# Moving one pair of pooled sums to GpSimd and reordering the hand-over to the second recurrence of a recommender kernel

## The chip, the cores and the metric

The kernel runs on one NeuronCore of a Trainium2 chip. The metric is device time in microseconds (us), from one launch; the times given are medians of several runs. A core has five engines with queues of their own, which run side by side and wait for one another through semaphores: TensorE (PE in the profile; PEld is its loading of weights), VectorE (DVE), ScalarE (ACT), GpSimd (POOL) and SyncE (SP, which here only issues DMAs).

## The reference

1024 sequences of 100 steps of 128 numbers pass a GRU; attention weights over its states pool them into one vector of 128 numbers for each sequence; then a second recurrence (AUGRU) runs over the GRU's states, and its update gate is scaled by numbers taken from the pooled vectors. Cut to what matters:

```python
_, gru_seq = jax.lax.scan(gru_step, h0, jnp.swapaxes(item_historical_embedding, 0, 1))
keys = jnp.swapaxes(gru_seq, 0, 1)
...
attn = jax.nn.softmax(score, axis=1)[..., 0]
pooled = jnp.einsum('bt,btd->bd', attn, keys)
att_seq = pooled.T[:T]

def augru_step(h, inp):
    x_t, a_t = inp
    ti = jnp.concatenate([h, x_t], axis=-1)
    r = jax.nn.sigmoid(ti @ aug_Wr.T + aug_br)
    u = jax.nn.sigmoid(ti @ aug_Wu.T + aug_bu)
    h_hat = jnp.tanh(jnp.concatenate([h * r, x_t], axis=-1) @ aug_Wh.T + aug_bh)
    u = a_t[:, None] * u
    h_new = (1.0 - u) * h + u * h_hat
    return (h_new, h_new)
_, aug_seq = jax.lax.scan(augru_step, h0, (jnp.swapaxes(keys, 0, 1), att_seq))
```

The state at each sequence's own last step, with other features, goes through a small network that gives one score for each sequence. Note `att_seq`: number t of a sequence's pooled vector is its weight at step t of the second recurrence. So the second recurrence needs the whole pooling finished, and then the pooled numbers by step instead of by sequence.

## The kernel before, in words

All is held in fp32. The 1024 sequences are worked on as two halves of 512; a tile is 128 partitions by 512 columns, and a matmul of 512 columns is issued as two instructions.

**First phase** (`gru_phase`). A loop over 100 steps does both halves of the GRU, the attention scores, a running softmax and the pooled sums. The states are written to `keys_d` in HBM, transposed in blocks of 32, as rows that can be gathered later: `keys_d[0]` has steps 0 to 3, `keys_d[1]` steps 4 to 11, and so on. `Half.pool(count, eng, cs)` (line 671) takes pending items of one half off its list `todo` and issues them on the engine `eng` for the columns `cs`: an item without a step rescales the sum (line 683), each other item is a pair, a product at line 693 and a sum at line 694. `count` limits the pairs.

The end of the phase (lines 1075 to 1145) is written out by hand, in the order in which the engines get it. The columns 0 to 3 of the pooled vectors (`soon`) are finished first, since steps 0 to 3 need them; from them, by matmuls, come `chosen` (the weights of those steps, sorted) and the first state `h3`. Then come the other 28 columns (`rest`): GpSimd does the rescaling and one pair of half 0 (line 1135); VectorE finishes half 1 (line 1137), SP issues four stores of its pooled rows to `pooled_d` (line 1140); then VectorE does half 0's last pair, and SP issues four stores of half 0. SP last issues a 1 MB store of half 0's keys (line 663), and GpSimd gathers the eight remaining blocks of half 0's key rows for steps 4 to 11 (`more_early`, line 193). A gather is an indirect DMA of 128 rows that GpSimd issues; each takes its queue's place.

**Second phase** (`augru_phase`, line 1147). It sits behind a branch on a value that was read from HBM. For each step t and half i, `half_step(t, i)` (line 1271) does this:

- PE: closes the `ph` gate of the half step before (line 1260, from `r`), closes `pr` and `pu` of its own, then opens `pr`, `ph`, `pu` of the half step after (line 1256, from the keys).
- ACT: tanh and two sigmoids (lines 1268, 1284, 1285).
- DVE: products with the other half's new state and with this half's gates (lines 1290, 1292, 1294, 1298, 1301).

PSUM banks are handed out by hand. The opened gates take them in turn from `ring`, which begins 6, 3, 1, 0, 2, 5, 4. One more bank (`pa`, a single buffer) serves transposes and other short matmuls. `SPARE` is bank 0.

What the first steps add:

- `chosen_rows` makes the weights of step 1; `store_chosen(i, p)` (line 1190) makes those of steps 0 to 3 in the bank `p`, ACT copies them (line 1193), SP stores them to `att_d` and loads the rows for steps 2 and 3 (line 1220). Both halves are called in `half_step(1, 1)`, half 0 in bank 0 and half 1 in `pa`.
- `load_key(t, i)` makes the keys of a step: for steps 1 to 3 by four transposes on PE into `pa` (line 1238) and a copy on ACT (line 1239), later by transposes on DVE (line 1245) from the gathered rows, which all have to be there.
- `gather_weights(i)` (line 1177): four gathers of sorted rows from `pooled_d` (line 158). They wait for all eight stores.
- `store_weights(i)` (line 1198), in `half_step(2, 1)` for half 0 and `half_step(3, 0)` for half 1: DVE multiplies the gathered rows by a mask (line 1203), PE transposes them into `pa` (line 1205), DVE copies them (line 1207), SP stores them to `att_d` and loads the row of step 4.
- From step 2 on, `load_att(t + 2, i)` and `load_key(t + 2, i)` run two steps ahead. `load_key(4, 1)` is issued in `half_step(3, 1)`, and PE opens the gates of (4, 1) in `half_step(4, 0)`.

GpSimd's queue in the second phase: four gathers of half 1's key rows for steps 4 to 11, the eight of the sorted weights, the other twelve of those key rows (three behind each half step of steps 1 and 2), then those for steps 12 and on. The last kind is paced: GpSimd copies one column of `rest` of the half step at hand (line 192) ahead of each gather.

Of the kernel before, what the change touches and what calls it, by code (L numbers as in the profile page):

```python
# [9 lines left out]
F32 = mybir.dt.float32  # L10
# [9 lines left out]
P = 128  # L20
B = 1024
T = 100
HB = 512
NH = B // HB
# [34 lines left out]
SOON = P // R  # L59
# [26 lines left out]
def kernel(ctx: ExitStack, tc: tile.TileContext, a: dict, out: bass.AP):  # L86
# [26 lines left out]
    nc = tc.nc  # L113
# [31 lines left out]
    used_s = const.tile([P, NH, GH, T - SOON], U8, name="used_s")  # L145
# [21 lines left out]
    def load_rows(q, i, width, tiles):  # L167

        n = READ[q]
        if q < WHOLE:  # L170
            r = rows[q, i] = tiles.tile([P, GH, n * P], F32, tag="once", name="rows")
            for g in range(GH):
                gather(r[:, g, :], keys_d[q], g, i)
                yield
            return

        parts, tag = (2, "kt") if tiles is kx else (1, "rows")
        some = [
            tiles.tile([P, KH // parts, n * R], F32, tag=tag, name="rows") for _ in range(parts)
        ]  # L180
        rows[q, i] = some
        for k in range(-(-width // R)):
            load_row(q, i, k)
            yield
# [19 lines left out]
    def gru_phase(pools):  # L204
# [36 lines left out]
        pa = pools.enter_context(tc.tile_pool(name="pa", bufs=2, space=PSUM))  # L241
# [508 lines left out]
        halves = [Half(i) for i in range(NH)]  # L750
# [173 lines left out]
        rest = load_later()  # L924
# [9 lines left out]
        for s in range(T):  # L934
            last = s == T - 1
            n, due = divmod(s - again, 4)
            n, i = divmod(n, NH)
# [137 lines left out]
        soon, rest = slice(0, SOON), slice(SOON, R)  # L1075
# [56 lines left out]
        halves[0].todo = late[0]  # L1132
        q = (T - 1) // G
        kept = halves[0].kt[q]
        halves[0].pool(1, nc.gpsimd, rest)
        for half in reversed(halves):
            half.pool(T, nc.vector, rest)
            to = pooled_d[half.cols, :].rearrange("(k r) f -> r k f", r=R)
            for p in range(P // R):
                nc.sync.dma_start(  # L1140
                    out=to[:, :, ts(p, R)], in_=pooled[ts(p, R), half.ks, :]
                )
# [4 lines left out]
    def augru_phase(pools, widths, alive):  # L1147
# [15 lines left out]
        pa = pools.enter_context(tc.tile_pool(name="pa3", bufs=1, space=PSUM))  # L1163
# [13 lines left out]
        def gather_weights(i):  # L1177
            r = wp.tile([P, GH, P], F32, tag="att_r", name="att_r", bufs=2)
            for g in range(GH):
                gather(r[:, g, :], pooled_d, g, i)  # L1180
            return r
# [8 lines left out]
        def store_chosen(i, p):  # L1190
            chosen_rows(i, p[:SOON, :], quad)
            rows_t = wp.tile([P, HB], F32, tag="att_t", name="att_t", bufs=2)
            nc.scalar.copy(rows_t[:SOON, :], p[:SOON, :])
            nc.sync.dma_start(out=att_d[i][:SOON], in_=rows_t[:SOON, :])
            for t in range(2, SOON):
                load_att(t, i)

        def store_weights(i):

            n = T - SOON  # L1200
            p = pa.tile([P, HB], F32, tag="a", name="pw")
            later_rows = sorted_rows[i][:, :, SOON:T]
            nc.vector.tensor_mul(later_rows, later_rows, used_s[:, i])
            for g in range(GH):
                nc.tensor.transpose(p[:n, ts(g, P)], sorted_rows[i][:, g, SOON:T], ident)
            rows_t = wp.tile([P, HB], F32, tag="att_t", name="att_t", bufs=2)
            nc.vector.tensor_copy(rows_t[:n, :], p[:n, :])
            nc.sync.dma_start(out=att_d[i][SOON:], in_=rows_t[:n, :])
            load_att(SOON, i)
# [14 lines left out]
        def load_key(t, i):  # L1224

            q = max(j for j, first in enumerate(FIRST) if first <= t)
            w, m, r = widths[t], t - FIRST[q], rows[q, i]
            if t >= one and i:
                k = keys.pop((t, 0))
            else:  # L1230
                k = qp.tile([P, HB], F32, name="k3")
            keys[t, i] = k
            if t >= one:
                k = k[:, ts(i, P)]
            if q < WHOLE:
                p = pa.tile([P, HB], F32, tag="a", name="pk3")
                for g in range(-(-w // P)):
                    nc.tensor.transpose(p[:, ts(g, P)], r[:, g, ts(m, P)], ident)
                nc.scalar.copy(k[:, :w], p[:, :w])
            else:  # L1240
                w, n = -(-w // R), KH // len(r)
                for j, part in enumerate(r):
                    u = min(w - j * n, n)
                    if u > 0:
                        nc.vector.transpose(
                            k.rearrange("p (k r) -> p k r", r=R)[:, j * n : j * n + u, :],
                            part[:, :u, ts(m, R)],
                        )

        def open_gates(t, i, names=("pr", "ph", "pu"), banks=(None,) * 3):  # L1250

            k = keys[t, i][:, : widths[t]]
            for name, n in zip(names, banks):
                m = {"pr": wr, "ph": wh, "pu": wu}[name]
                p = opened[t, i, name] = bank(name, n)[:, : widths[t]]
                nc.tensor.matmul(p, lhsT=m[:, 1, :], rhs=k, start=True, stop=False)  # L1256
# [14 lines left out]
        def half_step(t, i):  # L1271


            w, h = widths[t], h3[i][:, : widths[t]]
            before, after = ((t - 1, 1), (t, 1)) if i == 0 else ((t, 0), (t + 1, 0))
            if before in resets:
                open_state(*before)
            pr = close_gate(t, i, "pr", wr, h)
            pu = close_gate(t, i, "pu", wu, h)
            if t == 1:  # L1280
                row = pa.tile([P, HB], F32, tag="a", name="row")
                chosen_rows(i, row, quad[:, 1:2].to_broadcast([P, P]))
                open_gates(1, i, ("ph",), (None, LATE_BANKS[2])[1 - i :])
            nc.scalar.activation(pr, pr, AF.Sigmoid, bias=later["br"])
            nc.scalar.activation(pu, pu, AF.Sigmoid, bias=later["bu"])
            if t == 1:
                first_weights(i, row)
            state = states.pop(1 - i, None)
            if state is not None:
                nc.vector.tensor_mul(state[0], state[0], state[1])  # L1290
            r = wp.tile([P, HB], F32, name="r3")[:, :w]
            nc.vector.tensor_mul(r, h, pr)
            if state is not None:
                nc.vector.tensor_sub(state[3], state[0], state[2])
            if (t, i) == (1, 1):
                store_chosen(0, bank("spare", SPARE))
                store_chosen(1, pa.tile([P, HB], F32, tag="a", name="spare"))
            nc.vector.tensor_mul(pu, pu, att.pop((t, i))[:, :w])
            rest = wp.tile([P, HB], F32, name="rest")[:, :w]

            nc.vector.scalar_tensor_tensor(  # L1301
                out=rest, in0=pu, scalar=1.0, in1=h, op0=ALU.subtract, op1=ALU.mult
            )
            later["pace"] = rest[:, 0:1] if t > SOON - 2 else None
            resets[t, i] = r, pu, rest
            if t == 1:
                load_key(2, i)
            if (t, i) == (1, 0):
                open_gates(1, 1, ("pr", "pu"))
            elif after[0] < min(T, one) and (*after, "pr") not in opened:  # L1310
                open_gates(*after)
            elif after[0] == one < T:
                open_both(one, "pr", "pu", "ph")
            if (t, i) == (1, 1):
                load_key(3, 0)
            elif (t, i) == (2, 0):
                load_key(3, 1)
            elif (t, i) == (2, 1):
                store_weights(0)
            elif (t, i) == (3, 0):  # L1320
                store_weights(1)
            if SOON - 2 < t < T - 2:
                load_att(t + 2, i)

            if t == FIRST[1] - 1:
                load_key(t + 1, i)
            if (t, i) == (FIRST[1], 1):
                load_key(t + 1, i)
            if FIRST[1] - 2 < t < T - 2 and (t, i) != (FIRST[1] - 1, 1):
                load_key(t + 2, i)  # L1330
# [204 lines left out]
        chosen = [later["chosen", i] for i in range(NH)]  # L1535
        keys.update({(1, i): later["key", 1, i] for i in range(NH)})
        open_gates(1, 0, ("pr", "pu"), LATE_BANKS)
        ahead = load_rows(1, 1, widths[FIRST[1]], kp)
        for _ in range(P // R):
            next(ahead)  # L1540
        sorted_rows = [gather_weights(i) for i in range(NH)]
        due = spread_over(-(-widths[FIRST[1]] // R) - P // R, NH * (FIRST[1] - 2))
        jobs, final = [], None
        for t in range(1, T):
# [145 lines left out]
```

## Time and profile before

| | |
|---|---|
| runs | 1997.23 us median of 3 (1996.26 to 1997.49) |
| profiled execution | 1999.16 us, of which the span from first to last instruction is 1997.4 us |
| PE | busy 1981.9 us, 99% of the span |
| DVE | busy 1675.5 us, 84% |
| POOL | busy 1262.1 us, 63% |
| ACT | busy 942.0 us, 47% |
| granted TensorE clock | 0.998 of full speed on average |

The first phase's last work on DVE ends at 1417.14 us of the span; the first result of the second phase there starts at 1417.92 us. The times below are us from the span's start. A row of the timeline gives start, duration, engine, line, operation, output and inputs, shape and count, and in brackets how long the engine was idle before it and what released it. A row of the chain of waits gives start, duration and what was then on the path that ended last; "issue" is time in which the engine waited for nothing that the profile shows.

### The profile page before, as it was taken

The numbers are of one execution on the slowest core, as the hardware profiler recorded it, in microseconds if no ns is written. First come the engines' busy times: TensorE is split into PE (matmuls) and PEld (weight loads), VectorE is DVE, ScalarE is ACT, GpSimd is POOL, SyncE is SP. The second block draws the span as 40 slices with busy tenths as digits, with TensorE's granted clock in tenths as the row PEclk, the third lists the DMA queues.
The fourth block names the chain that finished last, engine by engine and source line by source line (L and its number), as shares of the span: only waits on it lengthen the run. The fifth ranks groups of instructions, "written<-read, shape, count | busy, mean of one in ns | idle before, by whom it ended". The sixth has DMA issues, their size and how long they took to land.

```text
span 1997.4 us, 40939 instructions
## 1 busy us (share of the span) xinstructions
PE 1981.9 (99%) x15324; PEld 943.8 (47%) x15324; DVE 1675.5 (84%) x3040; ACT 942.0 (47%) x1691; POOL 1262.1 (63%) x1298
## 2 busy tenths in 40 slices
PE   9999999999999999999999999999999999999998
PEld 2344444444333333333333333334444556678997
DVE  7888999888979888888888798999677778888995
ACT  4444454454544444544545444446434444445553
POOL 0333949659796959596796858898763354445331
PEclk9999999999999999999999999999999999999999
DMA  4443333233334434332343333232543333333331
GB/s 125 99 118 92 108 99 101 90 89 109 116 100 117 116 99 134 109 106 83 106 128 108 92 107 108 92 107 67 157 142 93 96 110 96 93 104 100 83 82 36
DMA packets 244573, 205.60 MB, mean 103 GB/s; under 512 B 61811, under 2 KB 207068, under 8 KB 244364
## 3 DMA queue, kind: packets, MB, share of 16 engines
q1 hardware_dynamic: 231852, 170.31, 30.1%
q0 software_dynamic: 12224, 32.05, 5.6%
q8 instruction: 122, 2.00, 0.4%
q14 instruction: 87, 0.71, 0.1%
q10 hardware_dynamic: 288, 0.52, 0.1%
HBM read 146.75 MB, written 54.42 MB: 101 GB/s over the span
## 4 chain that ended last, share of the span: by engine, by line
PE 97%; DVE 1%; ACT 1%; issue 0%; DMA 0%; POOL 0%; DVEq 0%; ACTq 0%; POOLq 0%
PE ps L588 51%; PE pm L764 18%; PE ph L1260 5%; PE pr L1260 4%; PE pu L1260 4%; PE ph L1256 4%; PE pu L1256 4%; PE pr L1256 4%; PE pr L1349 0%; PE last L731 0%; PE ph L1349 0%; PE p L1469 0%; ACT pr L1368 0%; PE pd L248 0%; DVE r L1376 0%
## 5 line engine op out<-in xcount | busy, mean ns | idle before, releaser
L588 PE MATMUL ps<-x,wih 128*32 128x512 f32 x4800 | 775.1, 593 | 0.0
L588 PE MATMUL ps<-hn,whh 128*32 128x512 f32 x4752 | 768.5, 592 | 1.3 <-ACT hn L636 1.3
L588 PEld LDWEIGHTS ps<-x,wih 128*32 128x32 f32 x4800 | 237.8, 110 | 318.0 <-issue 314.1
L588 PEld LDWEIGHTS ps<-hn,whh 128*32 128x32 f32 x4752 | 235.4, 110 | 314.9 <-issue 309.4
L600 ACT ACTIVATE r<-ps,brz 128x512 f32<-128x512 f32 x200 | 137.6, 688 | 382.1 <-PE ps L588 382.0
L573 POOL TENSOR_TENSOR xm<-x,m 128x512 f32<-128x512 f32 x200 | 233.8, 1169 | 64.7 <-DMA m<-mask_d 64.3
L574 POOL TENSOR_TENSOR hist<-hist,xm 128x512 f32<-128x512 f32 x200 | 258.5, 1292 | 15.7
L193 POOL DMA_INDIRECT rows<-keys_d,idx_k x218 | 212.2, 973 | 84.8 <-POOL rows L192 70.0
L764 PE MATMUL pm<-hn,wk 128*32 128x512 f32 x1200 | 257.0, 592 | 0.0
L764 PE MATMUL pm<-kq,wkq 128*32 128x512 f32 x1200 | 256.9, 592 | 0.0
L694 POOL TENSOR_TENSOR pooled<-pooled,kw 128x512 f32<-128x512 f32 (+1 forms) x191 | 244.6, 1281 | 15.0
L693 POOL TENSOR_TENSOR kw<-kt,e 128x512 f32<-128x512 f32 (+1 forms) x191 | 205.3, 1075 | 69.1 <-DVE e L882 69.0
L619 ACT ACTIVATE ps<-ps,bih 128x512 f32<-128x512 f32 x200 | 132.4, 662 | 226.5 <-DVE ps L618 225.6
L1268 ACT ACTIVATE c<-ph,bh 128x510 f32<-128x510 f32 (+57 forms) x174 | 88.1, 506 | 255.9 <-PE ph L1260 255.7
L608 DVE SCALAR_TENSOR_TENSOR u<-ps,bhh,r 128x512 f32<-128x512 f32 x198 | 147.5, 745 | 71.3 <-PE ps L588 68.9
L764 PE MATMUL pm<-mv,w 128*32 128x512 f32 (+1 forms) x808 | 194.2, 592 | 0.0
L623 DVE TENSOR_TENSOR d<-hn,ps 128x512 f32<-128x512 f32 x198 | 136.0, 687 | 35.8 <-ACT ps L619 35.4
L636 ACT COPY hn<-ps 128x512 f32<-128x512 f32 x200 | 116.4, 582 | 95.4 <-DVE kq L630 93.7
L624 DVE TENSOR_TENSOR d<-ps,d 128x512 f32<-128x512 f32 x200 | 138.3, 691 | 27.0 <-ACT ps L620 12.5
L618 DVE TENSOR_TENSOR ps<-ps,u 128x512 f32<-128x512 f32 x200 | 140.0, 700 | 21.5 <-DVE u L608 0.5
L192 POOL COPY rows<-rest 128x1 f32<-128x1 f32 x186 | 34.9, 188 | 194.4 <-DVE rest L1301 192.7
L1290 DVE TENSOR_TENSOR pu<-pu,c 128x510 f32<-128x510 f32 (+57 forms) x173 | 81.8, 473 | 76.5 <-ACT c L1268 74.5
(268 smaller groups left out, 3159.1 us busy)
## 6 DMA issues: line engine op xcount, KB each, us to landing
x<-in_hist_x SPq DMA_DIRECT2D x210, 256.0 KB
keys_d<-kt SPq DMA_DIRECT2D x48, 1024.0 KB
m<-mask_d SPq DMA_DIRECT2D x200, 128.0 KB
rows<-keys_d,idx_k POOLq DMA_INDIRECT x218, 2.9
s_b<-mv SPq DMA_DIRECT2D x200, 8.0 KB
keys_d<-kt SPq DMA_DIRECT2D x32, 64.0 KB
mask_i<-in_mask SPq DMA_DIRECT2D x8, 200.0 KB
part_d<-part SPq DMA_DIRECT2D x2, 400.0 KB
```

The lines of the kernel that those rows point to most:

```text
L193: nc.gpsimd.indirect_dma_start(out=r[:, at, :], out_offset=None, in_=keys_d[q], in_offset=bass.IndirectOffsetOnAxis(ap=idx_k[:, k, i : i + ...
L573: nc.gpsimd.tensor_mul(d, x, m)
L574: nc.gpsimd.tensor_add(acc, acc, d)
L588: nc.tensor.matmul(p[ts(q, R), :], lhsT=w[:, g, ts(q, R)], rhs=v, start=(j == 0), stop=(j == len(parts) - 1),)
L608: nc.vector.scalar_tensor_tensor(out=u, in0=ph, scalar=bhh[:, 2:3], in1=r, op0=ALU.add, op1=ALU.mult,)
L618: nc.vector.tensor_add(pi, pi, u)
L624: nc.vector.tensor_mul(d, pz, d)
L693: eng.tensor_mul(d, k, w)
L694: eng.tensor_add(acc, acc, d)
L764: nc.tensor.matmul(p[i][s, :], lhsT=w[:, s], rhs=v, start=start, stop=stop)
L1256: nc.tensor.matmul(p, lhsT=m[:, 1, :], rhs=k, start=True, stop=False)
L1260: nc.tensor.matmul(p, lhsT=m[:, 0, :], rhs=v, start=False, stop=True)
```

## The change

Four edits, none of which adds or removes arithmetic:

```diff
-        halves[0].pool(1, nc.gpsimd, rest)
-        for half in reversed(halves):
+        halves[0].pool(T, nc.gpsimd, rest)
+        for half in halves:
             half.pool(T, nc.vector, rest)
             to = pooled_d[half.cols, :].rearrange("(k r) f -> r k f", r=R)
             for p in range(P // R):
...
+        def mask_weights(i):
+            later_rows = sorted_rows[i][:, :, SOON:T]
+            nc.vector.tensor_mul(later_rows, later_rows, used_s[:, i])
+
         def store_weights(i):
...
-            later_rows = sorted_rows[i][:, :, SOON:T]
-            nc.vector.tensor_mul(later_rows, later_rows, used_s[:, i])
...
             if (t, i) == (1, 1):
                 store_chosen(0, bank("spare", SPARE))
-                store_chosen(1, pa.tile([P, HB], F32, tag="a", name="spare"))
...
             resets[t, i] = r, pu, rest
+            if t == 2:
+                mask_weights(i)
             if t == 1:
                 load_key(2, i)
...
             if (t, i) == (1, 1):
+                store_chosen(1, pa.tile([P, HB], F32, tag="a", name="spare"))
                 load_key(3, 0)
...
         open_gates(1, 0, ("pr", "pu"), LATE_BANKS)
+        sorted_rows = [gather_weights(i) for i in range(NH)]
         ahead = load_rows(1, 1, widths[FIRST[1]], kp)
         for _ in range(P // R):
             next(ahead)
-        sorted_rows = [gather_weights(i) for i in range(NH)]
```

1. Half 0's last pair of the 28 columns (one product, one sum) goes from VectorE to GpSimd. The stores to `pooled_d` are issued for half 0 first and half 1 second.
2. GpSimd issues the eight gathers of sorted weights ahead of the first four key gathers of the second phase.
3. The mask products (line 1203) move from `store_weights` to the end of the half steps (2, 0) and (2, 1), a half step sooner for each half.
4. In `half_step(1, 1)` the second call of `store_chosen` moves behind `load_key(2, 1)` and the opening of the gates of (2, 0), ahead of `load_key(3, 0)`.

## Prediction

> **What bounds the kernel now.** I read the engines' busy times first, then the chain of waits from 1385 to 1470 us, where the two phases meet, then the timelines of POOL, DVE and PE there, then the table of windows for the granted clock. The page says that PE is the bound:
>
> ```profile
> PE 1981.9 (99%) x15324; PEld 943.8 (47%) x15324; DVE 1675.5 (84%) x3040; ACT 942.0 (47%) x1691; POOL 1262.1 (63%) x1298
> ```
>
> So only PE's idle time and its slow stretches can be won, 15.5 us in all (1997.4 less 1981.9), plus what a low clock costs inside the busy time. The change touches the stretch from 1403 to 1457 us. In the chain of waits (start, duration, what) it is these places:
>
> ```profile
> 1416.52 0.62 DVE pooled L694
> 1417.14 0.14 DVEq L1609
> ...
> 1417.92 0.70 DVE r L1292
> 1418.62 0.04 issue
> 1418.66 1.58 PE ph L1260 x2
> 1420.24 1.70 PE pr L1260 x2
> 1421.94 1.25 PE pu L1260 x2
> ...
> 1426.75 0.58 ACT att_t L1193
> 1427.34 0.04 issue
> 1427.38 0.66 PE pk L1238 x4
> ...
> 1441.63 0.51 issue
> 1442.14 0.61 PE pw L1205 x4
> ...
> 1447.82 0.56 issue
> ```
>
> First DVE holds up PE (PE's row at 1418.66 has 2.09 us of idle time before it, put down to DVE's r); then three gates take 1.58, 1.70 and 1.25 us where the same gates take 0.85 each at 1431; then a 0.67 us wait for ACT's copy; then 0.51 and 0.56 us in which PE waits for the mask product. The windows show why the gates are slow (columns: window, its length, busy time of PE, PEld, DVE, ACT, POOL, granted clock, DMA share, GB/s):
>
> ```profile
> 1415.78:1419.19 3.41, 1.32 (x3) 0.30 (x2) 2.52 (x4) 0.00 (x0) 2.70 (x3) 1.00 0.85 170
> 1419.19:1422.60 3.41, 3.41 (x6) 1.35 (x5) 1.41 (x3) 1.31 (x2) 2.03 (x3) 0.50 1.01 212
> 1955.09:1958.50 3.41, 2.67 (x24) 2.52 (x22) 2.58 (x14) 1.88 (x7) 2.22 (x4) 1.00 0.39 94
> 1989.22:1992.63 3.41, 1.92 (x14) 1.35 (x18) 0.36 (x2) 1.25 (x4) 0.00 (x0) 1.00 0.06 20
> 1992.63:1996.05 3.42, 0.84 (x8) 0.00 (x1) 0.42 (x1) 0.00 (x0) 0.00 (x0) 0.50 0.05 13
> ```
>
> On this grid of 3.41 us a window with 1.32 or 1.92 us of PE work is followed by half clock, one with 2.67 us is not. So about 1.5 us of idle time in one window halves the clock in the next, and 0.74 us doesn't.
>
> **The pair on GpSimd.** DVE loses one product and one sum (128x448, 0.63 and 0.62 us); in the chain 1415.79 to 1417.14, 1.35 us. Half 1's last sum still ends at 1415.75, so r starts at 1416.57 and PE resumes at 1417.31: its idle time falls from 2.09 to 0.74 us. **-1.35 us.** The window then holds 2.67 us of work, as the third row above, and keeps the clock: the three gates go from 4.53 to 2.55 us. **-1.98 us**; nothing, where a run before had kept its clock.
>
> POOL gains a product (1.02 us) and a sum (1.14 us) with 0.1 us between, from 1406.9 to 1409.2. Behind them wait the eight key gathers, now 1407.08, needed by DVE only at 1449.63: free. DVE's 448-column rows take 0.62 us beside POOL's work (1405 us) and without (1414 us), so I charge nothing there. SP issues half 0's stores at 1409 us, half 1's from 1415.78 for 1.96 us (the row of the first four), and is done at 1417.74 instead of 1420.24. Its 1 MB store of keys also goes 2.5 us sooner; nobody waits for it.
>
> By the Trainium skill, "TensorE: Matmul & The Clock Gate", section "Why this matters for your kernels", only idle gaps over some 3 us cost the clock. The 2.09 us gap here did it already, so the measurement decides. By the rule the 1.98 us would not be won, nor a stall of 1.6 us punished, and the sum below would be -0.6 us.
>
> **The second chosen weights.** Nothing vanishes. The 0.67 us wait for ACT's copy out of `pa` now falls on `load_key(3, 0)` instead of `load_key(2, 1)`. Opening pr of (2, 0) uses bank 0, the next of the ring, which is `SPARE`; it now comes one group of transposes (0.44 us) behind half 0's matmul, while ACT's copy out of that bank takes 0.57 us and two handovers. **+0.2 us**, between -0.65 (the wait vanishes) and +0.67 (a second full wait). On ACT the second copy stands behind the copy of the keys of (2, 1) (0.58 us), which is over before PE's three opened gates (2.55 us) are. SP's store and its two loads for steps 2 and 3 of half 1 (1428.85, 1431.86) move back by those gates and forward by the 3 us that PE is early, so they stay where they are.
>
> **The masks.** PE no longer waits for line 1203: 0.51 and 0.56 us. **-1.07 us.** The products (0.55 us) fill idle time of DVE, 2.05 us ahead of 1438.16 and 0.88 us ahead of 1444.36. The new wait is DVE's, at about 1433, for the sorted weights; behind it stand all of DVE's products and so PE. Half 0's gathers end at about 1425 and land 2.5 to 4.3 us later: 4 us of cover; beyond that it would cost us for us.
>
> So PE comes to the gates of (4, 1) early by 1.35 + 1.98 - 0.2 + 1.07 = 4.2 us.
>
> **The gathers.** This is where I think the gain goes.
>
> ```profile
> 1424.12 0.94 POOL L158 DMA_INDIRECT att_r<-pooled_d,idx  x1 [2.29 <-issue]
> ...
> 1448.17 0.95 POOL L193 DMA_INDIRECT rows<-keys_d,idx_k  x1 [0.30 <-DVE rest L1301]
> ```
> ```profile
> 1454.00 0.70 DVE L1245 STREAM_TRANSPOSE k<-rows 128x512 f32<-128x512 f32 x1
> ```
> ```profile
> 1456.34 0.99 PE L1256 MATMUL pr<-k,wr 128*128 128x496 f32 x2
> ```
>
> A gather takes a slot of 1.25 us. Before, four key gathers (1417.13 to 1421.83) lay in the time that POOL waits for the stores anyway, and behind the wait came 20 gathers; the last started at 1448.17 and landed after 3.9 us, 1.9 us ahead of DVE's use at 1454.00. Now POOL has done its earlier work at 1419.3 and stands idle until the stores land, and all 24 come behind. The wait ended 3.88 us behind the last store's issue (1420.24 to 1424.12); with that, the first weight gather starts at 1421.6, at the least at 1419.3; with half the stores in the queue I take 1421.0. The last key gather then starts at 1421.0 + 24.05 + 4 x 1.25 = 1450.05, 1.9 us later than now, while DVE and PE come 4.2 us sooner. Gathers in this part land after 2.7 to 3.9 us; those issued at 1452.47, 1454.85 and 1456.30, under the burst of five loads that SP issues from 1452.71, took 4.8, 5.9 and 4.8 us. That burst follows half 1's `store_weights` and so moves to about 1448.5, onto the last two gathers: I take 4.8 us, with 2.7 and 5.9 as ends. Landing at 1454.85, 0.70 us of transposes and 0.15 us of handovers make the keys ready at 1455.7. PE would open the gates at 1456.34 - 4.2 = 1452.14: it stands for **+3.56 us** (1.46 to 4.66). That is over 1.5 us in one window, so the next runs at half clock, at the price that the same event has above: **+1.98 us**. Behind it nothing else is late: POOL's paced gathers waited 0.71 and 1.74 us for DVE at 1454 and 1459, so it catches up.
>
> **Sum:** -1.35 - 1.98 + 0.2 - 1.07 + 3.56 + 1.98 = +1.3 us on a profiled execution of 1999.16 us. The median of the runs is 1.93 us below that, 1997.23; the same difference on it gives 1998.5 us.
>
> **The rivals.**
> - Stall without low clock (0.25): the last gathers miss the burst and land after 2.7 to 2.9 us; PE stands for 1.5 us, at the edge of what the windows tolerate: -4.2 + 1.5 = -2.7, 1994.5 us. For it speaks that most gathers land so; against it, the burst.
> - Keys in time (0.08): the stores land at once, POOL starts at 1419.3, everything is won: -4.2, 1993.0 us.
> - Nothing moves (0.10): DVE's start in the second phase hangs on something other than the pair (0.78 us ahead of r is put down to a DMA), the clock still falls; then PE is early by the masks alone, 1.07 - 0.2 = 0.9 us, of which the keys at 1455.7 take 0.2 us back: 1996.5 us.
> - Slower (0.06): the same stall, with the keys at 1458.6 or later. From a landing time of 7.7 us (or a first weight gather at 1424) the stall of 6.4 us and the low clock outweigh the 4.2 us by over 4 us: 2001.5 us. Against it: no gather here took over 5.9 us.
> - Forecast, stall and low clock: 0.51.
>
> **Numbers.** 1998.5 us; with landings of 3.9 to 5.9 us the forecast's own range is 1997.7 to 1999.6, and a first gather at 1421.6 adds 0.6. The range 1994.3 to 2000.2 takes in the stall without low clock and the case in which nothing moves, and leaves out the two ends. A measurement of this kernel can tell about 0.2%, 4 us, from no change: faster 0.08, same 0.86, slower 0.06.
>
> **What would show it.** Idle time ahead of `ph` at the start of the second phase near 0.74 us, and clock 1.00 behind it; no idle time ahead of the `pw` transposes; `pk` of step 3 waiting for `att_t`; DVE waiting at line 1245 for a gather, near 1450, with PE idle ahead of `pr` of (4, 1), and 0.50 in a window behind it. I am wrong if that stall is missing or under 1.5 us, if the weights start well ahead of 1421, or if DVE waits at line 1203.

## The result and the profile after

The changed kernel takes 2001.33 us (median of 22 runs, 1999.24 to 2003.14), the kernel before 1996.92 us beside it (22 runs, 1996.06 to 1999.46): ratio 1.0019, 95% interval 1.0013 to 1.0025. The forecast was 1998.5 us, the end of its range 2000.2. The profiled execution took 2000.72 us (span 1998.9). Its first phase happens to be 1.9 us shorter (half 1's last pooled sum ends at 1413.84 us, at 1415.75 before), so all that follows counts from that sum's end.

The chain of waits of the changed kernel (start, duration, what):

```profile
1415.33 1.12 PE ph L1262 x2
1416.46 0.85 PE pr L1262 x2
1417.31 0.85 PE pu L1262 x2
...
1425.30 0.58 ACT att_t L1193
1425.92 0.67 PE pk L1240 x4
1426.60 0.27 issue
1426.86 0.94 POOL att_r L158
...
1448.28 0.95 POOL rows L193
...
1449.70 5.01 DMA rows<-keys_d,idx_k
1454.74 0.72 DVE k L1247
1455.51 2.02 PE pr L1258 x2
1457.53 1.60 PE ph L1258 x2
1459.13 0.83 PE pu L1258 x2
```

At its start the chain does as predicted: PE resumes 1.49 us behind the sum (2.91 before) and the three gates take 2.82 us in place of 4.53. ACT's copy still holds up one `pk`; the waits ahead of `pw` are gone. But from 1426.86 us the chain is no longer PE's. For 28 us it runs through GpSimd's row of gathers, each 0.95 us and 0.30 us of "issue", then through a landing, then VectorE. Before, it ran through PE there. (The view hangs the landing on the gather at 1449.70; the one that VectorE needs is that at 1448.28, which landed at 1454.62. The other landed at 1455.48, behind the transposes.)

The timeline rows of PE and VectorE in the changed kernel that carry the loss:

```profile
1455.51 2.02 PE L1258 MATMUL pr<-k,wr 128*128 128x496 f32 x2 [4.90 <-DVE k L1247]
```
```profile
1454.74 0.71 DVE L1247 STREAM_TRANSPOSE k<-rows 128x512 f32<-128x512 f32 x1 [6.54 <-DMA rows<-keys_d,idx_k]
```

SyncE's burst, five loads of attention rows (`at`), has moved as well. Its row in the kernel before stands 4.54 us behind the start of the last key gather (1448.17 us):

```profile
1452.71 2.23 SPq L1220 DMA_DIRECT2D at<-att_d  x5
```

In the changed kernel it stands 1.21 us ahead of that gather's start (1448.28 us):

```profile
1447.07 2.22 SPq L1222 DMA_DIRECT2D at<-att_d  x5
```

The table of windows of the changed kernel (window, length, busy time of PE, PEld, DVE, ACT, POOL, granted clock, DMA share, GB/s):

```profile
1414.57:1417.99 3.42, 2.74 (x7) 1.25 (x7) 2.68 (x4) 1.33 (x2) 1.89 (x2) 1.00 0.91 178
1448.70:1452.12 3.42, 1.91 (x5) 0.57 (x3) 0.00 (x0) 1.97 (x3) 2.87 (x5) 1.00 0.90 252
1452.12:1455.53 3.41, 0.02 (x1) 0.03 (x1) 0.79 (x2) 0.00 (x0) 2.57 (x6) 1.00 0.79 276
1455.53:1458.95 3.42, 3.42 (x4) 1.49 (x5) 3.39 (x7) 0.00 (x0) 1.11 (x2) 0.50 0.28 85
```

The half clock is gone from the start and is back behind the stall: there the three gates take 4.45 us, against 2.76 us at full clock in a variant below, so 1.69 us.

**One measure for all profiles.** From the end of half 1's last pooled sum to the start of the 21st product `pu<-pu,c` behind it the work is the same in every variant, but for e7's five extra matmuls. The kernel before takes 112.14 us for it, the changed one 115.02: +2.88 us. Its parts: PE reaches the gates of (4, 1) after 36.77 us instead of 40.59 (-3.82), stands for 4.90 us and pays 1.69 us of half clock; 0.1 us is left over. Each stretch is that of one profiled execution. The whole time is less sharp: in the profiles compared below, half 1's last pooled sum ends anywhere from 1413.84 to 1419.24 us, and what follows the stretch takes 468.9 to 470.2 us.

### The profile page after: what moved, and what is told of

Same layout as the page of the kernel before. It is cut to its first block, busy times and chain, and to the rows that moved or that the text cites. A ratio compares the mean times of both kernels' runs of the same rounds, so it can differ in the third digit from the quotient of the medians.

```text
span 1998.9 us, 40933 instructions
## 1 busy us (share of the span) xinstructions
PE 1981.0 (99%) x15324; PEld 1203.3 (60%) x15324; DVE 1673.1 (84%) x3038; ACT 941.8 (47%) x1691; POOL 1262.7 (63%) x1300
## 4 chain that ended last, share of the span: by engine, by line
PE 96%; DVE 1%; POOL 1%; DMA 1%; issue 1%; ACT 0%; SPq 0%; DVEq 0%; ACTq 0%; POOLq 0%
PE ps L588 51%; PE pm L764 18%; PE ph L1262 4%; PE ph L1258 4%; PE pr L1258 4%; PE pu L1262 4%; PE pu L1258 4%; PE pr L1262 4%; POOL rows L193 1%; PE pr L1353 0%; PE last L731 0%; PE ph L1353 0%; DMA rows<-keys_d,idx_k 0%; DMA item<-in_item 0%; PE p L1473 0%
## 5 line engine op out<-in xcount | busy, mean ns | idle before, releaser
L588 PE MATMUL ps<-x,wih 128*32 128x512 f32 x4800 | 789.4, 592 | 0.0
L588 PE MATMUL ps<-hn,whh 128*32 128x512 f32 x4752 | 784.0, 592 | 1.4 <-ACT hn L636 1.4
L588 PEld LDWEIGHTS ps<-x,wih 128*32 128x32 f32 x4800 | 321.5, 110 | 220.9 <-issue 148.2
L588 PEld LDWEIGHTS ps<-hn,whh 128*32 128x32 f32 x4752 | 319.3, 110 | 217.7 <-issue 155.7
L764 PE MATMUL pm<-hn,wk 128*32 128x512 f32 x1200 | 268.7, 592 | 0.0
L764 PE MATMUL pm<-kq,wkq 128*32 128x512 f32 x1200 | 268.6, 592 | 0.0
L694 POOL TENSOR_TENSOR pooled<-pooled,kw 128x512 f32<-128x512 f32 x192 | 245.3, 1277 | 15.1
L693 POOL TENSOR_TENSOR kw<-kt,e 128x512 f32<-128x512 f32 x192 | 206.2, 1074 | 68.0 <-DVE e L882 67.9
```

The costliest lines, as they stand in the source:

```text
L588: nc.tensor.matmul(p[ts(q, R), :], lhsT=w[:, g, ts(q, R)], rhs=v, start=(j == 0), stop=(j == len(parts) - 1),)
L693: eng.tensor_mul(d, k, w)
L694: eng.tensor_add(acc, acc, d)
L764: nc.tensor.matmul(p[i][s, :], lhsT=w[:, s], rhs=v, start=start, stop=stop)
```

## The experiments

**Theory:** the last key gather lands late because SyncE's burst of attention rows, pulled ahead by the change itself, shares the DMA engines with it. (On the scale of the profile before, the burst goes from 1452.71 to 1448.98 us and the gather from 1448.17 to 1450.19: the change moves both.) **Rivals:** the gather merely starts too late; the row of gathers is slow at its end whatever runs beside it; a cost in PE's or VectorE's order. All ratios are to the kernel before, run beside the variant. In the sets of e5 to e8 and e13 to e18 that kernel took 1999.2 to 1999.4 us, more than beside the changed kernel, so variants of different sets are compared by the stretch.

| run | burst starts, us behind the last key gather | landing | PE's wait | half clock behind it | stretch | ratio (95%) |
|---|---|---|---|---|---|---|
| changed kernel | -1.21 | 6.3 | 4.90 | yes | 115.02 | 1.0019 (1.0013 to 1.0025) |
| e13, three loads in place of five | -1.35 | 6.0 | 5.02 | yes | 114.77 | 1.0013 (1.0004 to 1.0022) |
| e15, gather order alone | -0.24 | 5.3 | 2.88 | no | 113.60 | 1.0011 (1.0002 to 1.0020) |
| e14, without gather order, weights split | +0.03 | 5.4 | 2.68 | yes | 112.13 | 0.9995 (0.9986 to 1.0005) |
| e5, without gather order | +1.07 | 2.8 | 0 | no | 108.18 | 0.9981 (0.9972 to 0.9990) |
| e6, pair alone | +2.15 | 3.7 | 0 | no | 109.04 | 0.9988 (0.9979 to 0.9997) |
| e17, burst later | +2.94 | 3.2 | 1.78 | no | 110.23 | 0.9991 (0.9982 to 1.0000) |
| kernel before | +4.54 | 3.9 | 0 | no | 112.14 | 1 |
| e18, all in time | +5.19 | 2.9 | 0 | no | 107.48 | 0.9987 (0.9978 to 0.9996) |
| e16, second chosen weights alone | +6.45 | 4.0 | 0 | no | 112.75 | 0.9997 (0.9988 to 1.0006) |

The stretch of the kernel before and of e16 has the half clock at its start in it.

**Without the order of the gathers** (e5):

```diff
-        sorted_rows = [gather_weights(i) for i in range(NH)]
         ahead = load_rows(1, 1, widths[FIRST[1]], kp)
         for _ in range(P // R):
             next(ahead)
+        sorted_rows = [gather_weights(i) for i in range(NH)]
```

> The change without its second edit, a second time: in the runs before this, ScalarE stood still for 2 to 8 us at a time between instructions that wait for nothing the profile shows, in the first 35 us behind the branch, in every kernel, so that those times say little of the change. Where those stops are missing, my theory (key rows of step 4 late through the order of the gathers, plus half clock) gives 1 us under to 3 us under the kernel before, with PE idle 0 to 1.5 us ahead of the gates of (4, 1). Rival A (the pair on GpSimd is the loss): 3 us or more above the kernel before.

The stall and its half clock vanish, and 6.84 us of the stretch with them. Four key gathers are back in the time in which GpSimd waits for the stores; the rest follows. It takes 4.1 us less than the kernel before beside it, more than the 1 to 3 us expected, and beats both kernels.

**The pair alone** (e6: edit 1 on the kernel before).

> The kernel before with the first edit alone, a second time, for the same reason. Where ScalarE's stops are missing: my theory 2 to 4 us under the kernel before (idle time at the start of the second phase 0.7 instead of 2.1 us, no half clock behind it, the keys of (4, 1) at most 1 us late). Rival A: 1 us or more above it. Rival C (the half clock there is chance): 1 to 1.5 us under it.

Stretch 109.04 us, -3.10; ratio 0.9988 (0.9979 to 0.9997), 2.7 us under the kernel before, as expected. The stretch is the idle time won at the start (1.40) and the three gates (1.71), nearly to the hundredth. Rival A doesn't fit. Rival C is half right: whether the 2.1 us gap halves the clock depends on where it falls (see e15 below), but in all 13 profiled executions with edit 1 the clock stays full at these gates.

**The order alone** (e15: edit 2 on the kernel before, the same lines as in e5 the other way round).

> The kernel before with the second edit alone, a third time. Where ScalarE's stops are missing: 4 to 6 us above the kernel before, with PE 2.5 to 4 us idle ahead of the gates of (4, 1) and half clock behind it. Rival D (the time of the stores makes the keys late, not the order): within 1 us of it.

A landing of 5.3 us and a stall of 2.9 us arise without any of the gains; but the loss is half of what was expected (1.9 us in the medians), and the stretch grows by 1.46 only. The half clock is missing twice. At the start this execution has the 2.10 us gap ahead of `ph` and yet keeps full clock, since the gap falls across two windows (1.87 and 0.23 us); that saves 1.7 us. And the stall falls across two windows too (1.18 and 1.70 us), with full clock behind it. Timeline rows of PE in it:

```profile
1419.43 1.12 PE L1260 MATMUL ph<-r,wh 128*128 128x510 f32 x2 [2.10 <-DVE r L1292]
...
1458.45 1.10 PE L1256 MATMUL pr<-k,wr 128*128 128x496 f32 x2 [2.88 <-DVE k L1245]
```

**The second chosen weights alone** (e16: edit 4 on the kernel before).

> The kernel before with the fourth edit alone. My theory: PE's wait of 0.67 us moves from one group of transposes to the next, and 0.1 to 0.2 us come on for the copy out of the bank that pr of (2, 0) takes: 0 to 0.3 us above the kernel before, no difference that can be told. Rival (the wait goes): 0.6 us under it.

Ratio 0.9997 (0.9988 to 1.0006), no difference that the runs can tell. The stretch of the one profile says 112.75 us: +0.6.

**Work in the stall** (e7): five matmuls that nobody reads, ahead of the gates of (4, 1), in the changed kernel (`filler`, not shown, issues them into `pa`).

```diff
             elif after[0] < min(T, one) and (*after, "pr") not in opened:
+                if (t, i) == (4, 0):
+                    filler(5)
                 open_gates(*after)
```

> The changed kernel with five more matmuls of 512 columns, whose result nobody reads, ahead of the gates of (4, 1): they fill 4.3 us of PE's stall there and take nothing from the arithmetic. My theory (the stall costs its length and then 1.8 us through the half clock): the stall stays, the half clock goes, the time is 1.3 to 2 us under the changed kernel's, i.e. some 2 to 3 us above the kernel before. Rival E (the half clock costs nothing, since DVE or ACT bounds the steps behind the stall): as the changed kernel, 4 us above the kernel before.

PE's row there is

```profile
1456.92 1.10 PE L1258 MATMUL pr<-k,wr 128*128 128x496 f32 x2 [0.92 <-DVE k L1247]
```

The first of the gates takes 1.10 us, at full clock, where it took 2.02. VectorE still waits for the gather, so the stall itself stays; ratio 1.0010 (1.0001 to 1.0019), stretch 113.65, 1.37 us under the changed kernel's although the gather took 6.65 us to land, 0.31 us longer. So the half clock is worth 1.4 to 1.7 us, and the stall the rest. The whole times can't say so: e7's median, 2001.24 us, is that of the changed kernel, whose runs stand beside a kernel before that was 2.2 us faster.

**Plain loads in place of the weight gathers** (e8):

```diff
-            for g in range(GH):
-                gather(r[:, g, :], pooled_d, g, i)
+            nc.sync.dma_start(
+                out=r, in_=pooled_d[ts(i, HB), :].rearrange("(g p) f -> p g f", p=P)
+            )
```

> The changed kernel with the eight gathers of sorted weights taken off GpSimd: SP reads the same number of pooled rows by two plain loads instead, so the weights are not sorted (this part of the computation is changed). My theory: GpSimd's key gathers follow one another from the end of its sums and the last starts near 1437 us of the span, far ahead of its use; no stall, and all that the other edits win stays: 3 to 4.5 us under the kernel before. Rival A (pair) or D (order of the stores): still 2 us or more above it.

Stretch 108.17 us, ratio 0.9982 (0.9973 to 0.9991). The last key gather starts at 1439.09 and nothing waits. The runs are 4.1 us under the kernel before, as expected. With e5 this shows that all the loss hangs on that gather, not on the order of PE's or VectorE's work; between lateness and slow landing it does not decide.

**Three loads in the burst** (e13: buffers of the attention rows from six to four in the changed kernel, here and in one more line).

```diff
-                at = wp.tile([P, HB], F32, name="at", bufs=6)
+                at = wp.tile([P, HB], F32, name="at", bufs=4)
```

> The changed kernel with four instead of six buffers for the attention rows, a second time. Where ScalarE's stops are missing: if the burst of loads makes the long landing of the last key gather (6.3 us), it falls to 4 to 5.3 us and the time is 1 to 2.3 us under the changed kernel's, 2 to 3 us above the kernel before. Rival (the burst is harmless): landing over 5.8 us, 3.5 to 4.5 us above the kernel before.

A miss: landing 6.0 us, stall 5.0 us. The number of loads is not what sets it, or at least not between three and five. This spoke for the rival (a row of gathers slow at its end), until the next runs. But three loads are still a burst, and one can be enough: in e5, far from the burst, the gather at 1446.63 us stands 0.26 us behind a single load of 248 KB and took 5.05 us; in e14 one at 1441.82, 0.08 us behind a single load, took 5.3.

**A version meant as the best** (e14: without edit 2, and the second chosen weights between the openings of `pr` and of the other two gates).

```diff
+            if (t, i) == (1, 1):
+                open_gates(2, 0, ("pr",))
+                store_chosen(1, pa.tile([P, HB], F32, tag="a", name="spare"))
+                open_gates(2, 0, ("ph", "pu"))
...
-                store_chosen(1, pa.tile([P, HB], F32, tag="a", name="spare"))
```

> The change without its second edit and with the second store_chosen between the openings of pr and of ph and pu, a second time. Where ScalarE's stops are missing: 4.3 to 5.3 us under the kernel before, PE's 0.67 us wait for ScalarE's copy gone. Rival (another wait takes its place): 3.5 to 4.2 us under it.

A miss: only 1.1 us under the kernel before. The wait for ACT goes (0.67 us), so PE is early, so SyncE's burst starts at 1448.10, exactly as the last gather does (1448.07): it lands after 5.4 us instead of 2.8, and 2.7 us of stall and a half clock cost more than the edit won. The same gather, the same place in the row, one us of difference to the burst.

**The burst alone moved** (e17: the changed kernel, half 1's store of sorted weights one half step later).

```diff
-            elif (t, i) == (3, 0):
+            elif (t, i) == (3, 1):
                 store_weights(1)
```

> The changed kernel with the store of half 1's sorted weights, and with it the loads of attention rows that follow it, one half step later (behind the half step of step 3's half 1 in place of half 0), so that the burst starts near 1452.6 us, 4 us behind the start of the last key gather (1448.3) and not 1.2 us ahead of it. First theory (the last gather lands late because it is issued beside the burst): it lands in 2.8 to 3.3 us, TensorE's wait ahead of the reset gates of step 4's half 1 falls from 4.9 to about 1.4 us, no half clock behind it, and the time falls by 3.5 + 1.8 = 5.3 us under the changed kernel's: 1995 to 1996.5, ratio to the kernel before 0.9985 to 0.9997. Rival (the last gather lands late because it stands at the end of a long row of gathers, whatever SyncE loads): it lands in 5 to 6.3 us, the wait stays 4 to 5 us, ratio 1.0010 to 1.0020. Second rival (the later loads are late for the update gates of step 4's half 1): VectorE waits on the attention rows there for 1 to 3 us, ratio 1.0000 to 1.0010.

This decides between the burst and the row. The gathers stand where the change put them, and the last one lands after 3.2 us. (The burst is four loads here; the next one follows at 1456.09 us.) Chain of waits of this variant:

```profile
1448.41 0.95 POOL rows L193
1449.36 0.30 issue
1449.66 3.23 DMA rows<-keys_d,idx_k
...
1453.02 0.72 DVE k L1247
...
1453.79 1.10 PE pr L1258 x2
1454.88 0.83 PE ph L1258 x2
1455.72 0.83 PE pu L1258 x2
```

GpSimd is still on the path (the gather is late), but the landing is 3.1 us shorter, PE stands for 1.78 us, and the clock stays; VectorE waits for no attention rows. So both causes have a size. Of the 6.84 us by which the changed kernel's stretch is over e5's, 4.79 go with the burst, and 2.05 stay here, where the gather is merely late. The slow landing has moved along with the burst: the gather issued at 1453.97, 1.4 us behind its start, takes 5.2 us. The DMA view of the time in which the gather is under way shows what shares the engines with it. The changed kernel, 1448.28 to 1454.62 us:

```profile
DMA packets 891, 1.77 MB, mean 279 GB/s; under 512 B 134, under 2 KB 759, under 8 KB 891
...
q1 hardware_dynamic: 703, 1.23, 65.6%
q0 software_dynamic: 188, 0.54, 23.5%
```

and this variant, 1449.66 to 1452.89 us (packets, MB, share of the 16 engines' time):

```profile
DMA packets 215, 0.48 MB, mean 148 GB/s; under 512 B 50, under 2 KB 50, under 8 KB 215
...
q0 software_dynamic: 103, 0.28, 26.8%
q1 hardware_dynamic: 112, 0.20, 25.2%
```

q0 carries the gathers, q1 SyncE's transfers. Beside the burst the loads have two thirds of the engines' time, the engines are busy for nine tenths of it, and the gather lands late.

**All in time** (e18): e14 and e17 together, and one key gather more ahead of the first phase's end, in a wait of GpSimd:

```diff
         stage()
+        gather_early(1)
         halves[0].pool(T, nc.gpsimd)
```

> The changed kernel with the sorted weights gathered behind the four key gathers again, the second chosen weights between the openings of the reset gates and of the other two of step 2's half 0, one more key gather early (in the 0.84 us in which GpSimd waits for the exponents of the last attention rows, so that all later gathers start 1.25 us sooner), and the store of half 1's sorted weights one half step later. The last key gather starts near 1446.8 us, ahead of any burst. First theory: no wait of TensorE over 0.7 us in the stretch from 1413 to 1460 us, landing of the last gather 2.8 to 3.2 us, so the time is that of the variant whose second chosen weights stand between the openings, less its stall and its half clock: 1998.35 - 2.7 - 1.8 = 1993.9, ratio 0.9970 to 0.9980. Rival (the landing is long at the end of the row of gathers whatever stands beside it): the gather lands near 1452.5 to 1453, a stall of 1.5 to 2.5 us stays, ratio 0.9982 to 0.9995.

The table of windows has PE without a gap where it stood before:

```profile
1440.00:1450.00 10.00, 10.00 (x28) 4.75 (x27) 8.22 (x15) 3.90 (x6) 7.68 (x10) 1.00 0.60 178
1450.00:1460.00 10.00, 10.00 (x25) 4.56 (x24) 8.49 (x15) 3.95 (x6) 8.17 (x14) 1.00 0.81 233
```

The stretch is the shortest of all, 0.70 us under e5, which is the wait that was taken out. The whole time, 1996.26 us, missed the expected 1993.9: its profiled execution spends 470.2 us behind the stretch (e5: 469.2), with the clock low for the last 8.5 us of the span (4.6 in e5). The intervals of e5 and e18 overlap; both beat both kernels, and which is better the whole times don't tell.

**Runs in which ScalarE stood still.** Two sets of runs had the kernel before itself at 2023.35 and 2019.73 us. Their variants tell little, and are only listed: without the gather order (e1) 1.0042 (1.0028 to 1.0055), the pair alone (e2) 1.0033 (1.0021 to 1.0045), the order alone (e3, e11) 1.0007 (0.9998 to 1.0016) and 1.0006 (0.9995 to 1.0017), the masks alone (e4, e12) 0.9980 (0.9971 to 0.9989) and 0.9980 (0.9969 to 0.9991), three loads (e9) 0.9977 (0.9968 to 0.9986), the version of e14 (e10) 1.0043 (1.0030 to 1.0057). Their order is nearly the reverse of that of the later sets. So the masks have no undisturbed run of their own. What was expected of the masks, which ran in these sets only, and of the pair:

> The kernel before with the third edit alone (mask products a half step sooner). My theory: PE's two waits of 0.5 us ahead of the transposes of the weights go, nothing new waits: 1995.6 to 1996.2 us, 0.7 to 1.3 us below the kernel before. Rival: the mask products make DVE wait for the gathers at step 2 and cost 1 us or more.

> The kernel before with the first edit alone (pair on GpSimd, stores of half 0 first). My theory: PE's idle time at the start of the second phase falls from 2.1 to 0.7 us and the half clock behind it goes; the keys of (4, 1) are ready at most 1 us late: 1993.5 to 1995.5 us. Rival A (the pair on GpSimd is the loss): 1998 us or more. Rival C (what the window of the clock does there is chance, not the gap): only 1.4 us are won, 1995.5 us or above.

Rows of ACT's timeline in e2:

```profile
1438.20 0.57 ACT L1193 COPY att_t<-spare 4x512 f32<-4x512 f32 x1 [7.80 <-remote]
1444.50 0.57 ACT L1193 COPY att_t<-spare 4x512 f32<-4x512 f32 x1 [5.73 <-remote]
1453.61 0.58 ACT L1239 COPY k<-pk 128x506 f32<-128x506 f32 x1 [8.54 <-remote]
```

The inputs of the first and the last of them had been ready for 5.9 and 7.4 us, and what released them ("remote") is nothing that the profile records. The stops end within 49 us of ScalarE's own branch (at 1406.67 us in e1, the last stop over at 1454.79), and none is in the profiles of the other sets. The Trainium skill, "Runtime: NRT & Kernel Launch", section "Instruction fetch mechanics", says that a taken branch to code not in the window stalls until it has been fetched. No run here shows a fetch of ACT's code at the stops: in e3 ScalarE branches at 1406.75 us, works on, and stands from 1437.77 to 1453.32 us, and in e2 the profile's queues of kind `instruction` move no packet from 1406 to 1470 us. The cause is open.

## Why the prediction was wrong

The mechanism was the one forecast: all gains come, then the last key gather takes back more than they are worth. Each step, in the stretch:

- **Idle time at the start:** predicted -1.35, measured -1.42. Right; e6 has it alone (-1.40).
- **The half clock avoided:** predicted -1.98, measured -1.71. The first of the three gates takes 1.12 us at full clock, not the 0.85 of the rows that were taken for it. The same slip is in the half clock behind the stall (+1.98, measured +1.69), so the two cancel.
- **The second chosen weights:** predicted +0.2, measured +0.6, by e16 and by the way from `row` (line 1184) to the closing of the `ph` gate of (1, 1), which takes 8.42 us instead of 7.83. As forecast, one wait of 0.67 us stays, now ahead of step 3's `pk`, and `pr` of (2, 0) comes some 0.25 us late behind ACT's copy out of its bank. The other 0.3 us had no term: they lie in the turns between groups of matmuls, of which there are more now, some 0.1 us at each.
- **The masks:** predicted -1.07, measured -1.29, which is only the rest of the 3.82 us: the wait and the handovers around it. Nothing waited at the new place.
- **Start of the weights and of the last key gather:** predicted 1421.0 and 1450.05, measured 1421.29 and 1450.20 on the scale of the profile before. Right.
- **The landing, the step that failed:** "I take 4.8 us, with 2.7 and 5.9 as ends"; it took 6.34. With it the stall is 4.90 us, not 3.56, and the steps come to +2.9 us in place of +1.3. The rows taken were right in kind (gathers beside the burst), but there were three of them, issued 0.24 us ahead of the first load and 2.14 and 3.59 us behind it; this one was issued 1.21 us behind it. In e5 the gather at 1453.04, 0.34 us behind the first load, took 7.2 us: the end of 5.9 was only what three rows happened to show. What sets the size between 5.2 and 7.2 us is open.
- **From profile to median, a second failure:** the steps give +2.9 us in the stretch, the medians +4.4. The prediction took off the same 1.93 us on both sides. But the profiled execution of before stood 2.2 us above the 22 runs' median, the profiled one after 0.6 us below its own. So that term was +0.6 us where -1.93 had been taken. In the later sets the kernel before took 1999.2 to 1999.4 us, as in its profile, and there the differences in the medians and in the stretch agree within 0.6 us for seven variants and within 1.6 us for the other three (e14, e16, e18). A part can be the half clock at the start. The prediction says that its 1.98 us are nothing where a run had kept its clock, but gave that no weight. Seven profiled executions have the start of the kernel before, with a gap of 2.1 us. In three (before, e3, e16) it lies in one window and half clock follows; in four (e4, e11, e12, e15) it is split by a window's end and the clock stays full. Where it stays, edit 1 wins 1.7 us less. Why the kernel before was 2.2 us faster in its first set stays open: the runs have no trace each, and the first phase alone differs by up to 5.4 us between profiles.
- **About 1.5 us of idle time in a window halves the clock:** too low for this part. 1.51 us in a window (the changed kernel, from 1448.70), 1.78 us (e17) and 1.87 us (e15) kept the clock, 2.09 us and 2.39 us (before, e14) lost it. The figure had come from a window near the end of the span.

Of the rivals, the one that ended slower had the right sign and nearly the right time (2001.5) by the same stall, but that is luck: it asked for a landing of 7.7 us and a stall of 6.4, and the 1.5 us between the stretch and the medians made up the rest. The "stall without low clock" is what e17 makes of the change (stall 1.78 us, stretch 1.9 us under the kernel before's).

## What to carry to other kernels

When PE is made earlier, everything that PE's results trigger is earlier too: look up which transfers these start, and what then shares the DMA engines with the one transfer that can't move. If a gather has to land in a given microsecond, move the burst rather than the gather; here one line did it. And a queue that waits anyway is a place for work that must be done sometime: the four gathers moved out of GpSimd's wait cost 5 us of its time later.

## What the runs showed of the hardware

- A gather of 128 rows landed after 2.5 to 4.1 us where SyncE issued no transfer from 3 us ahead of it until it landed, and after 5.2 to 7.2 us when it was issued between the first load of a burst and 2.6 us behind it, with three to five loads of 243 to 248 KB; issued 1.1 us ahead of the first load it took 2.8 us (e5). Right behind a single load it took up to 5.3 us (e14), and right behind the stores of pooled rows and of 1 MB of keys 5.5 us (e5, at 1421.50 us). How the engines divide their time between the two queues at that moment isn't settled here.
- On the 3.41 us grid, idle time up to 1.87 us (e15) in one window between 1413 and 1460 us kept full clock, and 2.09 us (the kernel before) did not. The Trainium skill, "TensorE: Matmul & The Clock Gate", section "Why this matters for your kernels", asks for gaps of no more than some 3 us. The measurements here decide for about 2 us, and for less later on: 1.78 us at 1900 us (e3) and, near the end of the span, 1.06 us (e17, e18) to 1.49 us (before) in a window were followed by half clock.
- Whether a gap of some 2 us costs 1.7 us depends on where it falls in the grid: the same gap ahead of `ph` was followed by half clock in three executions (2.09 to 2.13 us in one window) and not in four (split into 1.87 and 0.23 us in e15, 1.82 and 0.28 in e4, 1.76 and 0.34 in e11, 1.05 and 1.06 in e12).
- ScalarE can stand still, for up to 15.6 us at a time (e3) with its next input ready, in the 49 us behind its branch, in some sets of runs and not in others, and the kernel is then 20 to 26 us slower.
